# Seven block products in place of eight for some projections of a hybrid layer, with a later channel mix and a planner that tries several plans

## The chip, the cores and the metric

The kernel runs on one core of one Trainium2 chip. The metric is the device time of one execution in microseconds (us); lower is better. The profile comes from one execution, taken by the hardware profiler. TensorE is called PE (its weight loads PEld), VectorE DVE, ScalarE ACT, GpSimd POOL, SyncE SP.

## What is computed

Four stages, each added to its own input, on x of 4 batches x 1024 tokens x 256 features, all in fp32:

```
x = x + attention(layernorm(x))     # causal, one head of 256, softmax over 1024 keys
x = x + ffn(layernorm(x))           # channel mix: sigmoid(xr W_r) * (relu(xk W_k)^2 W_v)
x = x + state(layernorm(x))         # layernorm, W_in, a long convolution, silu gate z, W_out
x = x + ffn(layernorm(x))           # the same channel mix with the same weights
```

Two products matter here. In attention, the scores are (X Wm + bm) X^T, where Wm joins the weights of queries and keys; X Wm + bm are the "queries". In the state stage, z = silu(xn W_z + b_z), with W_z the second half of W_in; these are the "gates". Both are products of a 256 x 256 weight with a stream of tokens.

## The kernel before, in words

**Tiles.** A half batch j (0 to 7) is 512 tokens, a tile i (0 to 31) is 128. A stream of a half batch lies with features on partitions, in two blocks c of 128 x 512 (`cols`, L326). Tiles in SBUF come from a pool of 34 slots (L318); PSUM has 4 single banks ("bank", 128 x 512) and 2 pairs ("pair", 128 x 1024).

**The two products.** `project_columns` (L653) computes one output block e of a half batch: for c = 0, 1 one matmul of 128 x 128 weights with 128 x 512 of the stream, summed in one bank. `queries(j, e)` (L1163) evicts it with the bias on ACT or DVE; `state_gates(j, e)` (L1394) evicts it by one ACT instruction that adds the bias and applies silu. A whole batch takes two half batches x two blocks e x two c: eight matmuls. An fp32 matmul is recorded as two instructions, so x8 in the profile is four matmuls.

**The order is planned in Python.** `hybrid_kernel` does not emit instructions; it logs them in an `Order` (L49). A *unit* (`unit`, L86) is work of PE; units keep the order in which they are logged. Every other piece is an *op* (`op`, L72) with a list of engines that may do it ("ways") and a cost for each: `dve(n)` (L267), `act(n)` (L271), constants for POOL (1.27 for an addition of 128 x 512, 1.05 for a product), `columns(n, k)` (L41) for PE. `finish` (L162) first works out when each op is due (`_due`, L96, from what PE will need), then plays the program through once: an op whose inputs are there is offered at a time put off by a share of its slack (SHARE 0.2, at most MARGIN 2.5, L65); `_first` (L208) picks the op that could start first, its due time breaking ties; `_way` (L201) picks the engine that ends first; `_step` (L218) emits it. So the instruction order of DVE, ACT, POOL and SP follows from the modelled costs. The model knows PSUM banks and the DMA queue, but not the SBUF slots.

**The loop.** For each tile i, the loop at L1627 logs scores (L1203) two or three tiles ahead; DVE takes the row minimum, ACT the exponents, a write and four reads through DRAM with a DVE transposition (`turn_by_dram`, L1253) turn them into prT; then `weigh(i)` (L1314) multiplies by the values on PE (tile po) and DVE adds the result to x. `attend_prepare(j)` (L1132) normalizes a half batch and turns it into xa, and the queries and values (L1179) of the next half batch stand in between. `mix_units(i)` (L1590) puts the first channel mix (class Mix, L685: `keys`, `gates`, `values`) of half batch j at tiles i = 8 + 4j to 10 + 4j; each `values` is followed by `state_prepare(j)` (L1346: a second normalization, four ACT instructions and two POOL additions, and the turn through DRAM).

**After the loop** (L1672 on) the rest of the mix (6 and 7), the loads of the decay rows (`load_decay`, L1463: 16 DMAs of 512 KB into tiles hk), the small inputs of the convolution (`state_inputs`, L1414), the convolution (L1478), a trip of its states through DRAM (`states_out`, `states_in`), the skip products (L1527) and outputs follow. `more_gates(n)` (L1664) puts n of the 16 gate units where the order wants PE work that waits for nothing: 1, 3, 5, 1, 1, 3 and 2 of them. `mix1.transpose(7)` and `state_transpose(7)` turn the last half batch on PE, because it is needed soonest.

Of the kernel before, what the change touches and what calls it, by code (L numbers as in the profile page):

```python
# [4 lines left out]

# [7 lines left out]
F32 = mybir.dt.float32  # L13
# [6 lines left out]
P = 128  # L20
# [16 lines left out]
RPAD = P + L  # L37
AHEAD_FROM = 4
TURNED_BY_DRAM = 2

def columns(n, k=1):  # L41

    return 2 * k * max(n * 0.845e-3, 0.19)
# [5 lines left out]
class Order:  # L49
# [15 lines left out]
    SHARE, MARGIN, FRONT = 0.2, 2.5, 12.0  # L65
# [96 lines left out]
    def finish(self):  # L162
        self.due = self._due()
        self.now = self.at = 0.0
        self.free, self.ready, self.offered = {}, {}, []
        self.queue = 0.0
        self.waiting = {}
        self.psum = {kind: [0.0] * k for kind, k in self.BANKS.items()}
        for n, e in enumerate(self.log):
            if e["kind"] == "op":  # L170
                self._enter(n)
            elif e["kind"] == "known":
                self._done(e["key"], e["time"])
            elif e["kind"] == "take":
                heapq.heappop(self.psum[e["takes"]])
            else:
                self._unit(e)
        while self.offered:
            self._step()
# [28 lines left out]
    def _first(self):  # L208

        if not self.offered:  # L210
            return math.inf, None
        start, _, _, k = min(
            (self._way(time, n)[1], self.due[n], time, k)
            for k, (time, n) in enumerate(self.offered)
        )
        return start, k

    def _step(self):  # L218
# [5 lines left out]
        emit()  # L224
# [10 lines left out]
    def _unit(self, e):  # L235
# [20 lines left out]
        e["emit"]()  # L256
# [19 lines left out]
def hybrid_kernel(  # L276
# [389 lines left out]

    def project_rows(key, w, src, g, needs):
# [268 lines left out]
    def state_weights():  # L936
# [34 lines left out]
        o.op("lnb_w", ["ln"], ("POOL", 0.3, spread))  # L971
        o.unit("pb_all", 0.45, ["w_in", "lnb_w"], biases, "bank")
# [190 lines left out]
    def queries(j, e):  # L1163
        if e == 0:
# [11 lines left out]
            frees="bank",  # L1176
        )
# [212 lines left out]

    def columns_of(j):
        return [f"h{j}.T{c}" for c in range(KC)]
# [190 lines left out]

    def both(unit, j):
        unit(j, 0)
        unit(j, 1)
# [3 lines left out]
    def mix_units(i):  # L1590


        j, k = divmod(i - 8, 4) if i < NI - 1 else (6, 0)
# [31 lines left out]
    steps_of_weights = state_weights()  # L1625
    scored, valued = -1, 0
    for i in range(-2, NI):  # L1627
        first, second = mix_units(i)
        while scored < min(i + (2 if i < AHEAD_FROM else 3), NI - 1):
            scored += 1  # L1630
            scores(scored)
            if scored >= TURNED_BY_DRAM:
                turn_by_dram(scored)
        for unit in first:
            unit()
        if 0 <= i + 1 < TURNED_BY_DRAM:
            turn(i + 1)
# [3 lines left out]
        if 0 < j < 2 * NB:  # L1641
            if k == 0 and j + 1 < 2 * NB:
                attend_prepare(j + 1)
            if k == (1 if i < AHEAD_FROM else 0):
                both(queries, j)
        while valued < min(i + (3 if i < AHEAD_FROM else 4), NI - 1):
            valued += 1
            values(valued)
        for unit in second:
            unit()  # L1650
        if i == 10:
            decay_powers([f"e{i}", "la", "dtc", "dtr"])
# [4 lines left out]
        if i >= 0:  # L1657
            weigh(i)
            if i % NH == NH - 1:
                mix1.prepare(i // NH, by_hand=i == NI - 1)  # L1660

    all_gates = iter([(j, e) for j in range(2 * NB) for e in range(KC)])

    def more_gates(n):  # L1664
        for _ in range(n):
            state_gates(*next(all_gates))
# [6 lines left out]
    load_decay(1, ["po31"])  # L1673
    both(mix1.gates, 6)
    more_gates(1)
    both(mix1.values, 6)
    state_prepare(6)
    mix1.transpose(7)
    more_gates(3)
# [9 lines left out]
    more_gates(1)  # L1689
# [4 lines left out]
    more_gates(1)  # L1694
# [6 lines left out]
    more_gates(3)  # L1701
    mix_states(0)
    more_gates(2)
# [86 lines left out]
```

## Time and profile before

| | |
|---|---|
| median of 3 runs | 472.55 us (471.34 to 472.76) |
| the profiled execution, its own time | 471.39 us |
| its span (first to last instruction) | 469.2 us |
| granted TensorE clock | 1.0 |
| instructions | 6471 |
| DVE busy | 335.0 us, 886 instructions |
| ACT busy | 190.6 us, 348 instructions |
| POOL busy | 110.0 us, 119 instructions |
| memory traffic | read 40.54 MB, written 28.45 MB |

The span is the time between the first and last instruction of the program; 2.2 us of the execution lie around it. Busy time of an engine is the union of its instructions. Matmuls overlap in the pipeline, so the mean duration of one is longer than the distance to the next.

### The profile page before, as it was taken

Reading aid. Unit: us, or ns where it says so; the run is one execution under the profiler, and the core shown is the slowest. Engines: PE = TensorE matmul, PEld = TensorE weight load, DVE = VectorE, ACT = ScalarE, POOL = GpSimd, SP = SyncE. Lnnn points to the kernel's source line nnn. Section 1 sums busy time; section 2 is a strip of 40 time slices with the busy share of each in tenths; the row PEclk is TensorE's granted clock in tenths of the full one; section 3 lists DMA queues with packets and bytes.
Section 4 is the critical chain, followed back from the end, with each engine's and each line's share of the span. In section 5 each row is a group of like instructions: output and inputs, shape, how many; then the busy total and the mean of one; then the engine's idle time right before and its main releaser. Section 6 shows DMA issues by size and latency. Waiting matters only on the chain.

```text
span 469.2 us, 6471 instructions
## 1 busy us (share of the span) xinstructions
PE 463.4 (99%) x2074; PEld 317.2 (68%) x2074; DVE 335.0 (71%) x886; ACT 190.6 (41%) x348; POOL 110.0 (23%) x119
## 2 busy tenths in 40 slices
PE   8999999999999999999999999999999999999996
PEld 5765775857867757866768756474565875877765
DVE  3678879589898897786897985411577984986642
ACT  3521333335235534537442585501113454345632
POOL 3000301112402503503322374300001310243330
PEclk9999999999999999999999999999999999999999
DMA  7047864844647854628883588903032241425312
GB/s 233 26 121 216 264 174 104 243 128 143 196 115 144 228 152 136 161 77 247 258 253 88 175 270 229 342 1 80 11 113 90 80 145 45 133 92 179 92 67 67
DMA packets 84914, 69.42 MB, mean 148 GB/s; under 512 B 20161, under 2 KB 82577, under 8 KB 84881
## 3 DMA queue, kind: packets, MB, share of 16 engines
q1 hardware_dynamic: 84064, 68.76, 49.7%
q8 instruction: 16, 0.26, 0.2%
q10 hardware_dynamic: 816, 0.26, 0.2%
q14 instruction: 18, 0.14, 0.1%
HBM read 40.54 MB, written 28.45 MB: 147 GB/s over the span
## 4 chain that ended last, share of the span: by engine, by line
PE 96%; DMA 1%; DVE 1%; ACT 0%; SPq 0%; issue 0%; DVEq 0%
PE sc L1217 13%; PE po L1322 13%; PE py L1534 6%; PE pv L1189 6%; PE pc L1484 2%; PE py L1546 1%; DMA wq<-in_L_attn_a_Wq_dram 1%; PE pb L1421 1%; PE pp_a0.pq L659 1%; PE pr_g1.pv L674 1%; PE pr_g0.pr L674 1%; PE pr_f4.pr L674 1%; PE pr_f3.pr L674 1%; PE pr_f2.pr L674 1%; PE pr_f1.pr L674 1%; PE pr_f0.pr L674 1%
## 5 line engine op out<-in xcount | busy, mean ns | idle before, releaser
L1322 PE MATMUL po<-v,prT 128*128 128x256 f32 x288 | 67.9, 380 | 0.4 <-DVE prT L1275 0.3
L1217 PE MATMUL sc<-xa,q 128*128 128x512 f32 (+3 forms) x192 | 67.0, 486 | 0.0
L1322 PEld LDWEIGHTS po<-v,prT 128*128 128x128 f32 x288 | 54.2, 190 | 11.1 <-issue 2.4
L1217 PEld LDWEIGHTS sc<-xa,q 128*128 128x128 f32 x192 | 35.2, 190 | 23.6 <-issue 18.7
L1238 ACT ACTIVATE pr<-pr,nmx 128x128 f32<-128x128 f32 (+7 forms) x32 | 24.7, 772 | 57.7 <-DVE pr L1233 55.5
L1189 PE MATMUL pv<-wv,xa 128*128 128x257 f32 x128 | 32.9, 380 | 0.0
L797 POOL TENSOR_TENSOR x<-x,r_g 128x512 f32<-128x512 f32 x14 | 20.1, 1432 | 51.7 <-DVE r_g L791 41.3
L543 POOL TENSOR_TENSOR rs_f<-ve_f,minus_half 128x4 f32<-128x4 f32 x8 | 8.3, 1037 | 99.3 <-DVE ve_f L530 99.3
L797 POOL TENSOR_TENSOR x<-x,r_f 128x512 f32<-128x512 f32 x16 | 20.3, 1271 | 42.9 <-DVE r_f L791 41.7
L1189 PEld LDWEIGHTS pv<-wv,xa 128*128 128x128 f32 x128 | 24.1, 191 | 7.8 <-issue 2.9
L1534 PE MATMUL py<-xnT,wk 128*128 128x512 f32 x64 | 28.8, 596 | 0.0
L1233 DVE TENSOR_SCALAR_CACHE_REDUCE pr<-sc,v 128x128 f32<-128x128 f32 (+7 forms) x32 | 26.2, 818 | 1.1
L1556 DVE SCALAR_TENSOR_TENSOR z<-py,b_skip,z 128x512 f32<-128x512 f32 x16 | 11.0, 742 | 22.2 <-PE py L1546 22.2
L1275 DVE STREAM_TRANSPOSE prT<-pblocks 128x384 f32<-128x384 f32 (+7 forms) x30 | 23.9, 797 | 3.2 <-DMA pblocks<-exps 3.0
L1332 DVE SCALAR_TENSOR_TENSOR x<-po,rsm,x 128x256 f32<-128x256 f32 x32 | 15.5, 484 | 12.4 <-PE po L1322 10.2
L543 POOL TENSOR_TENSOR rs_g<-ve_g,minus_half 128x4 f32<-128x4 f32 x8 | 8.6, 1078 | 58.3 <-DVE ve_g L530 55.8
L1366 POOL TENSOR_TENSOR x<-x,bout_r 128x512 f32<-128x512 f32 x16 | 20.4, 1286 | 8.1 <-ACT x L1359 8.0
L1534 PEld LDWEIGHTS py<-xnT,wk 128*128 128x128 f32 x64 | 12.0, 190 | 13.7 <-issue 13.0
L543 POOL TENSOR_TENSOR rs_h<-ve_h,minus_half 128x8 f32<-128x8 f32 x8 | 13.8, 1720 | 30.0 <-DVE ve_h L532 27.3
L1359 ACT ACTIVATE x<-x,mrs_h,rs 128x256 f32<-128x256 f32 x32 | 17.2, 590 | 2.9 <-DVE rsm L1331 2.9
L1199 DVE TENSOR_TENSOR v<-pv,bv_r 128x257 f32<-128x257 f32 x32 | 13.2, 414 | 6.9 <-PE pv L1189 6.6
L712 ACT ACTIVATE xk_g<-hT_g,muk 128x512 f32<-128x512 f32 x16 | 11.1, 715 | 16.6 <-DVE hT_g L616 16.6
(429 smaller groups left out, 949.9 us busy)
## 6 DMA issues: line engine op xcount, KB each, us to landing
hk<-r_dram SPq DMA_DIRECT2D x16, 512.0 KB, 8.3
rows_g<-xn_g SPq DMA_DIRECT2D x8, 512.0 KB, 3.1
blocks_g<-rows_g SPq DMA_DIRECT2D x32, 128.0 KB, 2.7
x<-in_L_attn_a_X_dram SPq DMA_DIRECT2D x7, 512.0 KB, 4.9
rows_f<-xn_f SPq DMA_DIRECT2D x7, 512.0 KB, 3.4
blocks_f<-rows_f SPq DMA_DIRECT2D x28, 128.0 KB, 2.8
rows_h<-xn_h SPq DMA_DIRECT2D x7, 512.0 KB
blocks_h<-rows_h SPq DMA_DIRECT2D x28, 128.0 KB, 3.5
```

The lines of the kernel that those rows point to most:

```text
L543: nc.gpsimd.tensor_tensor(rs()[:, :k].rearrange("p k n -> p (k n)"), ve()[:, :k].rearrange("p k n -> p (k n)"), minus_half[:, : k * NH], A ...
L674: nc.tensor.matmul(pr()[:, j, :], lhsT=src()[:, c, ts(2 * g + j, P)], rhs=w[:, c, :], start=(c == 0), stop=(c == KC - 1),)
L797: nc.gpsimd.tensor_add(xg, xg, r()[:, ts(g, 2), :])
L1189: nc.tensor.matmul(pv()[:, : D + 1], lhsT=xaj()[:, c, ts(n, P)], rhs=wv[:, c, :], start=(c == 0), stop=(c == KC - 1),)
L1217: nc.tensor.matmul(sc()[:, k * HALF : k * HALF + w], lhsT=qh()[:, c, ts(n, P)], rhs=keys[k]()[:, c, :w], start=(c == 0), stop=(c == KC - 1),)
L1233: nc.vector.tensor_scalar(dst, src, v[2 * b + h]()[:, n, D : D + 1], None, ALU.add, ALU.min, accum_out=nmx(),)
L1238: nc.scalar.activation(p()[:, :nk], p()[:, :nk], AF.Exp, bias=nmx(), scale=-1.0, accum_out=sm())
L1275: nc.vector.transpose(dst()[:, : NH * width].rearrange("p (k m a) -> p k m a", m=NH, a=GRP), blocks().rearrange("p m (k a) -> p k m a", a= ...
L1322: nc.tensor.matmul(po()[:, :D], lhsT=src()[:, ts(n, P)], rhs=v[2 * b + n // NH]()[:, n % NH, :D], start=(n == 0), stop=(n == t),)
L1359: nc.scalar.activation(xt, xt, AF.Identity, bias=mrs()[:, 0, n : n + 1], scale=rs1()[:, n : n + 1])
L1366: nc.gpsimd.tensor_add(xg, xg, bout_r.unsqueeze(1).to_broadcast([P, 2, D]))
L1534: nc.tensor.matmul(dst()[:, ts(e, HALF)], lhsT=w_x[:, c, ts(e, P)], rhs=src()[:, c, :], start=(c == 0), stop=False,)
```

## The change

A product of 2 x 2 blocks is done with seven block products (Strassen's scheme in Winograd's form) for the queries of batches 2 and 3 (`SEVEN_FROM = 2`) and the gates of batches 1, 2 and 3 (`PLAIN = 1`). Weight blocks A(e, c) and stream blocks B(c, h), with h the half of the batch, give four weight sums S (once, on DVE) and, for each batch, four stream sums T (POOL or DVE). Each product is one unit in one bank; its eviction adds it to what is already there. A sum takes p5 twice. For the gates, silu follows as an ACT instruction of its own in SBUF. Both halves of a batch have to be there, so the second half of batches 2 and 3 is prepared four tiles earlier (i = 8 and 16), beside the first. The seven query units are put one by one between other units (`go_on`, at least 0.8 us of other units apart) from i = 11 and i = 19, and are all logged before the batch's first scores.

The mix of half batch j moves from tiles 8 + 4j .. to 10 + 4j .., so `values` 5 and all of mix 6 come after the loop. The gate steps after the loop become 0, 0, 5, 3, 3, 7 and 7: four plain units and 21 products. The planner tries 20 plans (five pairs of share and margin, four values of `WAIT`), keeps the one whose modelled end is earliest, and lets an op with an earlier due time go first if it could start on the same engine within `WAIT`. The lower bound in `columns` falls from 0.19 to 0.105.

```diff
 def columns(n, k=1):
-    return 2 * k * max(n * 0.845e-3, 0.19)
+    return 2 * k * max(n * 0.845e-3, 0.105)
...
-    SHARE, MARGIN, FRONT = 0.2, 2.5, 12.0
+    PLANS = [
+        (share, margin, wait, change)
+        for share, margin in ((0.2, 2.5), (0.1, 1.5), (0.3, 4.0), (0.2, 1.5), (0.1, 2.5))
+        for wait in (0.0, 0.08, 0.15, 0.22)
+        for change in (0.0,)
+    ]
...
     def finish(self):
-        self.due = self._due()
+        self.dues = self._due()
+        ends = []
+        for plan in self.PLANS:
+            self._run(plan, False)
+            ends.append((max(self.now, *self.free.values()), plan))
+        self.ends = ends
+        self._run(min(ends, key=lambda end: end[0])[1], True)
...
+        first = min(ways)
+        due, _, start, k = min(
+            (w[1], w[2], w[0], w[3]) for w in ways
+            if w[0] <= first[0] + self.WAIT and w[4] == first[4]
         )
-        return start, k
+        if due < first[1]:
+            return start, k
+        return first[0], first[3]
...
+    def weight_sums(t, a):
+        nc.vector.tensor_add(t[:, 0], a(1, 0), a(1, 1))
+        nc.vector.tensor_sub(t[:, 1], t[:, 0], a(0, 0))
+        nc.vector.tensor_sub(t[:, 2], a(0, 0), a(1, 0))
+        nc.vector.tensor_sub(t[:, 3], a(0, 1), t[:, 1])
+
+    def stream_sums(key, src, needs):
+        t = [lazy(lambda k=k: cols(f"T{k}_{key}")) for k in range(KC)]
...
+        for k, plus, minus in (
+            (1, lambda: b(0, 1), lambda: b(0, 0)),
+            (3, lambda: b(1, 1), lambda: b(0, 1)),
+            (2, lambda: b(1, 1), lambda: sums(1)),
+            (4, lambda: b(1, 0), lambda: sums(2)),
+        ):
...
+            o.op(
+                f"{key}.T{k}", needs + ([f"{key}.T{k - 1}"] if k in (2, 4) else []),
+                ("POOL", 1.05, partial(emit, nc.gpsimd)), ("DVE", dve(HALF), partial(emit, nc.vector)),
+            )
...
+        p = unit(1, lambda: a(0, 0), lambda: src(0)[:, 0, :], there)
+        o.op(f"{key}.u1", [f"{key}.p1"], *copies(u, p), frees="bank")
+        yield
+        p = unit(2, lambda: a(0, 1), lambda: src(0)[:, 1, :], there)
+        add("c11", 2, p, u, block(0, 0), 0, ["u1"])
+        yield
+        p = unit(6, lambda: s_of(2), lambda: t_of(2), [f"{sums_key}.T2"])
+        add("u2", 6, p, u, block(0, 1), None, ["u1"])
+        yield
+        p = unit(7, lambda: s_of(3), lambda: t_of(3), [f"{sums_key}.T3"])
+        add("u3", 7, p, block(0, 1), u, None, ["u2", "c11"])
+        yield
+        p = unit(4, lambda: a(1, 1), lambda: t_of(4), [f"{sums_key}.T4"])
+        add("c21", 4, p, u, block(1, 0), 1, ["u3"])
+        yield
+        p = unit(5, lambda: s_of(1), lambda: t_of(1), [f"{sums_key}.T1"])
+        add("c22", 5, p, u, block(1, 1), 1, ["u3"], last=False)
+        add("v12", 5, p, block(0, 1), block(0, 1), 0, ["u3"])
+        yield
+        p = unit(3, lambda: s_of(4), lambda: src(1)[:, 1, :], there)
+        add("c12", 3, p, block(0, 1), block(0, 1), None, ["v12"])
+        yield
...
-        j, k = divmod(i - 8, 4) if i < NI - 1 else (6, 0)
+        j, k = divmod(i - 10, 4)
...
-            if k == 0 and j + 1 < 2 * NB:
-                attend_prepare(j + 1)
+            if k == 0 and j == 1:
+                attend_prepare(2)
+            for n in range(3, 2 * NB):
+                if i == 4 * n - (12 if n % 2 and n > 2 * SEVEN_FROM else 8):
+                    attend_prepare(n)
...
+    both(mix1.values, 5)
+    state_prepare(5)
+    more_gates(0)
+    mix1.keys(6, 0)
+    mix1.transpose(7)
+    mix1.keys(6, 1)
     both(mix1.gates, 6)
-    more_gates(1)
+    more_gates(0)
     both(mix1.values, 6)
     state_prepare(6)
-    mix1.transpose(7)
-    more_gates(3)
     both(mix1.keys, 7)
...
     more_gates(5)
     state_transpose(7)
     state_inputs(0)
-    more_gates(1)
+    more_gates(3)
...
     state_inputs_rows(1)
-    more_gates(1)
+    more_gates(3)
...
     skip(1)
-    more_gates(3)
+    more_gates(7)
     mix_states(0)
-    more_gates(2)
+    more_gates(7)
```

The helper `add` is one DVE instruction: `tensor_add` of the bank and an SBUF tile where no bias is given, else `scalar_tensor_tensor` (bank + bias + tile), with a cost of `dve(HALF) + 0.03`.

## The prediction, made before the change was run

> **What bounds the kernel now.** I read the page's busy shares first, then the chain that ended last, then that chain in order of time, then the windows.
>
> ```profile
> PE 463.4 (99%) x2074; PEld 317.2 (68%) x2074; DVE 335.0 (71%) x886; ACT 190.6 (41%) x348; POOL 110.0 (23%) x119
> PE 96%; DMA 1%; DVE 1%; ACT 0%; SPq 0%; issue 0%; DVEq 0%
> ```
>
> PE is busy 99% of the span and 96% of the last chain. A busy PE could still be a slow PE, and the Trainium skill says so: "Perfetto Trace Analysis", section "Identifying the Most-Contended Engine", calls matmul busy time a poor measure of the distance to the limit, for which the time in weight loads is the better one. By that rule PE stands at 68%, the most contended engine is DVE at 71%, and a change that takes matmuls away and gives DVE work gains nothing. The chain in order of time decides it (start, us, what):
>
> ```profile
> 138.89 3.43 PE pp_a5.pq L659 x8
> ...
> 263.34 3.45 PE pr_f6.pr L674 x16
> 266.80 1.72 PE pp_pz0.0_2455 L659 x4
> 268.51 3.45 PE pr_f6.pv L674 x16
> 271.97 0.87 PE pt_f7.hT L641 x8
> ...
> 295.20 1.72 PE pp_pz0.4_2681 L659 x4
> 296.92 1.24 PE pt_h7.T L641 x8
> 298.15 1.85 PE pb L1421 x16
> ```
>
> Each piece starts where the one before it ends, and a matmul instruction of 512 columns takes 3.43/8 = 1.72/4 = 0.429 us in every kind of unit, in attention and after it. So matmuls go through at a fixed rate whatever happens to the weight loads (0.19 us each, inside 0.429); I go by the row: a matmul less is time less, wherever PE is not made to wait. PE hardly waits for data now: outside the first 12 us I find 0.3 us at 65.2 (for prT) and 0.37 us in pt_h7 (1.24 us instead of the 0.87 of pt_f7).
>
> **What is removed.** Each batch done by seven products loses one matmul of 512 columns, that is two instructions: 2 x 0.429 = 0.86 us. Two batches of queries and three of gates: 5 x 0.86 = 4.29 us, all on the path. Nothing else of PE's work changes in amount; the mix, the preparation and the gates are moved.
>
> **What is added, and where.** These groups price it (busy, mean ns):
>
> ```profile
> L791 DVE SCALAR_TENSOR_TENSOR r_f<-r_f,pr_f3.pv 128x512 f32<-128x512 f32 x2 | 1.4, 690 | 1.4 <-PE pr_f3.pv L674 1.4
> L1577 DVE TENSOR_TENSOR x<-x,pr_pyo1.0_2971 128x512 f32<-128x512 f32 x1 | 0.7, 689 | 1.0 <-PE pr_pyo1.0_2971 L674 1.0
> L797 POOL TENSOR_TENSOR x<-x,r_f 128x512 f32<-128x512 f32 x16 | 20.3, 1271 | 42.9 <-DVE r_f L791 41.7
> ```
>
> - *Evictions.* Seven additions from a bank per batch, 0.69 us each: 4.8 us, 24 us for five batches, all on DVE. They replace two DVE evictions of queries (0.75 each). ACT gives up evictions and gets u1 and silu in SBUF: level. DVE goes to about 335 + 23 + weight sums (8 of 128x128, at 0.29 as the mask addition of that size, 2.3) = 360 us, 77%: no bound over the whole.
> - *Stream sums*, 20 of 128x512 with two SBUF inputs. The skill ("GPSIMD Engine Reference", section "Engine selection") says to keep elementwise additions on VectorE, GpSimd being about twice as slow. The row agrees in the ratio (1.27 us), but POOL is busy 23% of the time: on POOL they are 25 us that nothing waits for, on DVE 14 us more where it has least room. I go with POOL for most. The plan believes 1.05 us, so a T2, which follows T1, comes some 0.5 us later than planned; units p1 and p2 and those put between lie in front of p6.
> - *Banks.* Seven products in a row come every 0.86 us and are evicted at 0.69 us, with p5 evicted twice: 8 x 0.69 = 5.5 us against 6.0 us. Four banks cover the delay. In the stretch after the convolution DVE is nearly empty (below). Cost nothing; if DVE were 3 us behind there, banks would run out and PE would wait that long.
> - *Silu* now waits for a DVE addition instead of a product. Behind it in ACT's queue stand the normalizations of half batch 7 and the convolution's small work; ACT is busy 5.1 of 10 us at 290 to 300 and less after: 0 for those, and up to the lateness of that addition otherwise. Its table is still loaded once, since the gates come after the last exponential.
> - *Bound in `columns`, 20 plans.* They alter only orders, by a model. Between -0.3 us (the wait at 65.2 goes) and +1; I take 0.
>
> **Attention.** The windows of 10 us (columns: window and its length, PE, PEld, DVE, ACT, POOL, clock, DMA share and GB/s):
>
> ```profile
> 100.00:110.00 10.00, 10.00 (x26) 4.75 (x25) 9.22 (x15) 3.26 (x5) 1.90 (x1) 1.00 0.34 104
> 110.00:120.00 10.00, 10.00 (x107) 8.20 (x106) 9.37 (x33) 5.54 (x11) 1.02 (x1) 1.00 0.44 134
> ...
> 160.00:170.00 10.00, 10.00 (x34) 6.12 (x33) 9.30 (x20) 4.61 (x8) 1.46 (x2) 1.00 0.70 194
> ...
> 320.00:330.00 10.00, 10.00 (x29) 4.03 (x28) 2.73 (x4) 2.75 (x4) 0.00 (x0) 1.00 0.29 82
> ```
>
> The seven products of batch 2 fall at about 98 to 118 us, those of batch 3 at about 165 to 190. DVE is busy 27.7 of 30 us in 95 to 125 and 26.3 of 32 us in 163 to 195. To each comes 4.8 us of evictions and about 5.1 us of the earlier preparation (four statistics of 0.59, some of the normalizations at 0.42, two transpositions at 0.65, the small ones): 9.9 us. Over by 7.6 us and 4.2 us. What goes late first is what has room: prT. The DVE timeline and the chain show it for tile 13, the one with the least room of its neighbours:
>
> ```profile
> 108.86 0.96 DVE L1275 STREAM_TRANSPOSE prT<-pblocks 128x768 f32<-128x768 f32 x1
> ```
> ```profile
> 118.83 2.79 PE po L1322 x12
> ```
>
> Written at 109.8, first used at 118.8: 9 us; paired in the same way, tiles 12 to 31 have 5.9 to 15 us, and tile 15 (used at 131.8) 6.0. So 7.6 us of lateness fits but for 1.6 us if all of it falls on tile 15, and if the order puts evictions first, as due times from PE's needs do. Both ends: 0, or 7.6 + 4.2 = 11.8 us if no cover could be used. I take 0.2, near the lower end, because every row of cover is near or over the lateness. Queries must be complete before the scores of tiles 16 and 24; the last product is logged a tile ahead. The earlier preparation also takes one write and four reads past SP's queue and the DMA engines, at a DMA share of 0.34 to 0.44: hidden. The mix two tiles later takes its evictions, POOL additions and DMAs along, with inputs that are ready earlier than before: 0. The query weight sums (1.2 us of DVE near 22 us) stand before tiles 2 and 3, whose prT has 1.6 and 2.4 us of cover: 0; without it they would cost their 1.2.
>
> **After the loop** the filler changes, and this is where I expect to lose.
>
> - *pt_f7* needs the last tile's x, its statistics and POOL's power: inputs ready at 268.7, 5.3 us after the last po ended at 263.3. Before, 8.6 us of units lay between; now values 5 and half of keys 6, 3.45 + 1.72 = 5.2 us. Between 0 and 1.5 (values 5 bring DVE work into the gap): I take 0.2.
> - *pt_h7*: from the end of values 7 (288.3) to its inputs (297.2) are 8.9 us, against a filler of five gate units, 8.6 us: the 0.37 us above. Now four plain units and one product, 4 x 1.72 + 0.86 = 7.7 us: 0.86 us less. In the chain POOL's second addition waits 0.8 us behind another and the statistics 1.6 us behind two transpositions, so another order could save it. Between 0 and 1.2 (with T sums on POOL in front of its power): I take 0.5 more.
> - *h6*: `state_inputs(0)` needs the stream of half batch 6 through DRAM. Before, it was there at 292.9, 20.9 us after values 6 ended at 272.0, and needed at 298.1. Now values 6 come later: keys, gates and values 7 (10.3), the filler (7.7) and pt_h7 (0.9) leave 18.9 us, plus the waits above. That chain was put off by its slack before, but it shares the DMA queue with the 16 loads of hk (median 8.3 us to landing). Between 0 and 3: I take 0.3.
> - Behind the convolution the filler before `mix_states(0)` grows from 3.43 + 5.15 to 3.43 + 6.0 us: less exposed than now. Slots: not in the planner's model; four T tiles and one u come while hk holds 16, and z of batch 1 is not yet there. A wait for a slot would stop POOL first, which is idle at 310 to 330: 0.
>
> **Sum.** -4.29 + 0.2 + 0.2 + 0.5 + 0.3 = -3.1 us. The profiled execution took 471.39 us (span 469.2 and 2.2 around it), so 468.3 on its own terms, a span near 466.1. It lies 1.16 us under the median of 472.55, within the spread of the three; on the median, 469.5 us.
>
> **The rivals.**
> - *All of it arrives*, and the plan avoids the waits: 472.55 - 4.3 = 468.2. For it: PE had no waits before under the same model, and the best of 20 plans is taken. Against: the three gaps after the loop are shorter than the chains they cover.
> - *Given back after the loop*: pt_f7 1.5, pt_h7 1.2 and h6 1 to 3 at their upper ends, 3.7 and more: near 472.3, no change. For it: hk loads and half batches 5 and 6 share the queue and POOL. Against: each chain had idle time in it.
> - *DVE becomes the bound in attention, slower.* If bank evictions stand behind preparation work in DVE's order, PE's four banks fill and the lateness reaches PE. With 8 of the 11.8 us: 472.55 - 4.3 + 8 = 476.3. It turns the sign once more than 4.3 us reach PE, that is, when usable cover in each window falls from 6 us or more to under 3.7 (11.8 - 2 x 3.75 = 4.3). Against: prT's cover, and POOL for the sums.
> - *It doesn't do what it says*: a product of one matmul costing more than 0.43 per instruction for lack of accumulation; the transpositions and scores show no such price; included in the first range.
>
> **Chances.** Likeliest (469.5) 0.47; all of it 0.25; given back 0.13; slower 0.15. A measurement tells 0.3%, 1.4 us, from no change. Faster: 0.47 + 0.25 = 0.72; same 0.13; slower 0.15. The range reaches from the full gain with the waits of before gone and the runs' own spread of 1.2 under their median (466.8) to the lower half of the slower case (474.0), leaving out under 0.2.
>
> **What would show it.** Right: 80 matmul instructions of queries and gates fewer and 70 of products in their place, 2064 in all; PE busy near 459; waits in pt_f7 and pt_h7 of some tenths; DVE near 360 us with 90% and more at 95 to 195 and no PE wait there. Wrong: PE idle before po or a product's bank in 95 to 195 (rival three); pb waiting for `blocks_h` for microseconds (rival two); the additions on DVE well over 0.69 us; sums on DVE; a start-to-start of the products over 0.43 us.

## The result, and the profile after

| | before | after |
|---|---|---|
| median, same chip | 472.39 us (471.00 to 472.76, 5 runs) | 475.40 us (474.47 to 476.08, 5 runs) |
| ratio | | 1.0069, 95% interval 1.0047 to 1.0091 |
| the profiled execution, its own time | 471.39 us | 474.82 us |
| its span | 469.2 us | 473.0 us |
| granted TensorE clock | 1.0 | 0.992 |

The change is slower by 0.7%, 3.0 us, where 3.1 us of gain were forecast; the time lies outside the range of the forecast (466.8 to 474.0). The page of the kernel after: busy time, the granted clock in 40 slices of 11.8 us, and the shares of the chain that ended last.

```profile
PE 462.1 (98%) x2064; PEld 315.1 (67%) x2064; DVE 375.6 (79%) x931; ACT 192.7 (41%) x354; POOL 121.9 (26%) x128
...
PEclk9999999999999999999999998899999999999999
...
PE 74%; DVE 14%; DMA 6%; ACT 2%; issue 2%; SPq 1%; POOL 0%; DVEq 0%; ACTq 0%
```

PE had 96% of that chain before. Now DVE and DMA hold 20%, and the two slices from 284 to 307 us show a lower clock, just where PE stood still. The chain in order of time, at that place:

```profile
289.26 0.71 DVE xnT L651
289.97 0.89 DVE mrs_h L587 x2
290.87 0.62 DVE xnT L651
291.49 1.95 DVE xn_h L593 x2
...
293.48 1.54 PE pt_h7.T L676 x6
```

By the starts of its instructions, PE is idle from 288.23 to 292.30 and again from about 292.65 to 293.48, until half batch 7 is normalized. That takes three steps: POOL's power (`rs_h`, one over the root of the variances), DVE's shift (`mrs_h`, made of mean and power, 128 x 4) and the normalized rows (`xn_h`, 128 x 256 each). Before, they stood like this (timeline of before: start, us, engine, line, what):

```profile
294.33 1.65 POOL L543 TENSOR_TENSOR rs_h<-ve_h,minus_half 128x8 f32<-128x8 f32 x1 [1.90 <-DVE ve_h L532]
...
296.01 0.23 DVE L552 SCALAR_TENSOR_TENSOR mrs_h<-rs_h,mv_h 128x4 f32<-128x4 f32 x2 [1.76 <-POOL rs_h L543]
296.17 1.05 DVE L558 TENSOR_SCALAR xn_h<-x,mv_h,rs_h 128x256 f32<-128x256 f32 x3
```

From the powers' end (295.98) to the last normalized row: 1.2 us. After, the powers end at 288.33 and the rows are there at 293.43: 5.1 us. The timeline of after shows what stands between and what runs beside:

```profile
286.68 1.65 POOL L578 TENSOR_TENSOR rs_h<-ve_h,minus_half 128x8 f32<-128x8 f32 x1 [0.87 <-ACT z L1596]
...
288.30 1.26 POOL L1521 TENSOR_TENSOR x<-x,bout_r 128x512 f32<-128x512 f32 x1
289.26 0.71 DVE L651 STREAM_TRANSPOSE xnT<-blocks_h 128x512 f32<-128x512 f32 x1 [2.05 <-DMA blocks_h<-rows_h]
289.52 1.26 POOL L733 TENSOR_TENSOR T_zs<-xnT 128x512 f32<-128x512 f32 x1
289.90 0.97 DVE L587 SCALAR_TENSOR_TENSOR mrs_h<-rs_h,mv_h 128x4 f32<-128x4 f32 x2
290.74 1.26 POOL L733 TENSOR_TENSOR T_zs<-xnT,xnT 128x512 f32<-128x512 f32 x1
290.79 0.70 DVE L651 STREAM_TRANSPOSE xnT<-blocks_h 128x512 f32<-128x512 f32 x1
...
291.42 2.01 DVE L593 TENSOR_SCALAR xn_h<-x,mv_h,rs_h 128x256 f32<-128x256 f32 x2
...
291.97 2.59 POOL L1521 TENSOR_TENSOR x<-x,bout_r 128x512 f32<-128x512 f32 x2
292.30 0.66 PE L676 MATMUL pt_h7.T<-ident,xn_h 128*128 128x128 f32 x2 [3.91 <-DVE xn_h L593]
```

Two things make the 3.9 us more. First, DVE waits until 289.26 for the reads of half batch 6 through DRAM and transposes them (`xnT`, twice) in the order of its queue, ahead of the shifts and of the normalization: about 2.1 us that before had been over by then. Second, two shifts take 0.97 us instead of 0.23, and two normalizations 2.01 us where three took 1.05 (before, two of them took 0.73): about 2.0 us. Each of these two groups ends about when a POOL addition ends: 290.87 beside 290.78, 293.43 beside 293.3 (half of 2.59 from 291.97). Against this, 0.3 us are saved, since ACT normalizes one tile more. The same slowing shows at tile 31's half batch, before `pt_f7`:

```profile
258.52 1.26 POOL L924 TENSOR_TENSOR x<-x,r_f 128x512 f32<-128x512 f32 x1
...
258.60 1.20 DVE L587 SCALAR_TENSOR_TENSOR mrs_f<-rs_f,mv_f 128x4 f32<-128x4 f32 x1
```

**The ledger of the span** (after less before, from the starts of PE's instructions): five products less, -4.29; an earlier start of the first projection (11.68 instead of 12.38), -0.70; three old waits gone (65.2, 178 and the 0.37 in pt_h7), -1.0. Against it: 0.73 at 92.2 us (the first query product waits for DVE's transposition of xa), 0.73 at 114.5 (po13 behind DVE), 0.73 in pt_f7, 4.07 + 0.83 at the last transposition, and 2.7 of slow clock behind it (the convolution's inputs, pb, take 3.54 instead of 1.85 us in the chain). Sum: -6.0 + 9.8 = +3.8, for a measured +3.9.

### The profile page after: what moved, and what is told of

Its sections match the earlier page's. It is cut to its first block, busy times and chain, and to the rows that moved or that the text cites. A ratio compares the mean times of both kernels' runs of the same rounds, so it can differ in the third digit from the quotient of the medians.

```text
span 473.0 us, 6537 instructions
## 1 busy us (share of the span) xinstructions
PE 462.1 (98%) x2064; PEld 315.1 (67%) x2064; DVE 375.6 (79%) x931; ACT 192.7 (41%) x354; POOL 121.9 (26%) x128
## 4 chain that ended last, share of the span: by engine, by line
PE 74%; DVE 14%; DMA 6%; ACT 2%; issue 2%; SPq 1%; POOL 0%; DVEq 0%; ACTq 0%
PE po L1477 9%; PE sc L1372 9%; PE py L1729 6%; PE pv L1344 5%; PE p_zs L750 4%; PE p_qs L750 3%; PE pc L1679 2%; DMA blocks_h<-rows_h 1%; DMA rows_h<-xn_h 1%; DVE xr_f L842 1%; DVE pr L1388 1%; PE pb L1616 1%; DVE xk_f L842 1%; PE py L1741 1%; DMA wq<-in_L_attn_a_Wq_dram 1%
## 5 line engine op out<-in xcount | busy, mean ns | idle before, releaser
L578 POOL TENSOR_TENSOR rs_a<-ve_a,minus_half 128x4 f32<-128x4 f32 x7 | 7.1, 1010 | 65.7 <-DVE ve_a L565 65.7
L1521 POOL TENSOR_TENSOR x<-x,bout_r 128x512 f32<-128x512 f32 x16 | 20.7, 1309 | 8.1 <-ACT x L1514 8.1
```

What stands on the lines that cost most here:

```text
L578: nc.gpsimd.tensor_tensor(rs()[:, :k].rearrange("p k n -> p (k n)"), ve()[:, :k].rearrange("p k n -> p (k n)"), minus_half[:, : k * NH], A ...
L1521: nc.gpsimd.tensor_add(xg, xg, bout_r.unsqueeze(1).to_broadcast([P, 2, D]))
```

## Theories and experiments

**Theory H (holding).** A POOL addition that reads SBUF holds up DVE instructions that work between SBUF and SBUF; the change puts such additions (`shifted`, L1521, of half batches 5 and 6, and the new stream sums) where DVE normalizes the last half batches. **Rival W (work and order).** DVE merely has too much to do there, and the filler is shorter; POOL is a bystander. **Rival C (clock).** The wait is what it is, the low clock behind it makes the loss. I came to H only after the runs e1 to e8. Ratios are to before on the same chip.

**e1_dust and e2_filler: is it the filler or the clock?**

```diff
 # e1_dust
     more_gates(5)
+    keep_going(19)        # idle matmuls of 512 columns in bf16, at no cost in the plan
     state_transpose(7)
 # e2_filler: gate steps 0, 0, 9, 2, 2, 6, 6 in place of 0, 0, 5, 3, 3, 7, 7
```

> 19 idle bf16 matmuls of 512 columns (about 4 us of PE at full clock) stand ahead of the transpositions of half batch 7 (pt_h7), at a modelled cost of nothing, so that the order of all engines stays that of the changed kernel; they compute nothing that is used. Theory (a wait of 4.1 us at pt_h7 for the normalization of half batch 7, and after it a TensorE clock that has fallen because PE stood still, which costs about 3.4 us more between pt_h7 and the first product behind it): the wait is filled and not shortened, the clock stays at 1.0, and 2.5 to 3.4 us come back: 472 to 473 us. Rival (the slow stretch behind pt_h7 is data that comes late, not the clock): no change, 475.4 us, and the intervals of 0.83 us between pairs of the small products pb stay.

> Nine gate steps instead of five ahead of pt_h7, and 2, 2, 6, 6 behind in place of 3, 3, 7, 7: 3.4 us more of PE work that waits for nothing. The same arithmetic. Theory (filler shorter than the chain of half batch 7): the wait falls from 4.1 to under 1.5 us and the clock does not fall, 6 to 7.5 us come back: 468 to 469.5 us. Rival (DVE has too much work in this stretch, whatever the order of PE's units): the stream sums and evictions of the four products more come into the same stretch, the wait stays at 3 to 4 us: 474 to 476 us.

e1: 474.59 us, 1.0070 (1.0055 to 1.0085), as the change itself. The idle matmuls (4.26 us from 289.08) keep the clock at 0.998 and pb takes 1.92 us, yet PE then waits 0.9 us for `bT`, which stands on DVE behind four stream sums and starts at 299.98 (in after, behind the same sums, at 299.06). Nothing is won: the slow clock was spent in the shadow of a late DVE. C falls. e2: 477.91 us, 1.0153 (1.0110 to 1.0197), slower than both of its expectations; its trace is of an execution of 481.35 us. The wait at pt_h7 is gone, but the plan moved work and PE waits 5.8 us before pt_f7 and 2.2 before a product. More filler at one place isn't a cure.

**e3_sums: the stream sums at another place.** The sums of batch 1 are logged right behind the loop, those of batches 2 and 3 after the fifth product of the batch before.

> The stream sums of batch 1's gates are logged right behind the loop instead of with its first product, those of batches 2 and 3 after the fifth product of the batch before, so that they do not run while half batch 7 is normalized. Nothing else changes. Theory with contention (sums on POOL slow the normalizations on DVE to 1.0 us each from 0.42, and delay them): the wait at pt_h7 falls by 1 to 2 us, and with it some of the slow clock: 472 to 474 us. Theory without it (the chain is held up by DVE standing at the transposition of half batch 6 for its DMA): under 0.5 us, 475 us.

476.62 us, 1.0114 (1.0099 to 1.0129), no better than the change; the waits at the last transposition are 4.26 and 1.27 us. The sums alone are not it: with them away, three additions L1521 (290.30, 291.52, 292.75) lie on the shifts and the normalizations.

**e4 to e8: which part of the change loses?**

```diff
 # e4_order_alone: the later mix and the planner, no seven products
-PLAIN = 1
-SEVEN_FROM = 2
+PLAIN = 4
+SEVEN_FROM = 4
 # gate steps 0, 0, 5, 2, 2, 4, 3
 # e5_old_mix: all products, the order of before (mix at 8 + 4j), sums late, steps 1, 3, 10, 2, 2, 5, 2
 # e6_queries: the order of before, PLAIN = 4.   e8_gates: the order of before, SEVEN_FROM = 4
 # e7_plans_alone: the order of before, PLAIN = 4, SEVEN_FROM = 4
```

> The later mix, the new order behind the loop, the 20 plans and the new bound, but every projection with eight products: gate units 0, 0, 5, 2, 2, 4, 3 (16 plain ones). Theory (products only shorten the filler at pt_h7 and add sums there; the order would nearly do): against the kernel before, a wait of 0 to 2 us at pt_h7: 472.5 to 475 us. Rival (the seven products are the loss, the order none): 472 to 472.8 us. Other rival (the later mix alone makes the loss, since half batch 6 then runs into half batch 7): the same wait of 3 to 4 us and the slow clock: 478 to 480 us.

> All seven-product batches, the 20 plans and the new bound, but the channel mix at tiles 8 + 4j and the order behind the loop as in the kernel before (mix 5 and half of mix 6 inside the loop); gate steps 1, 3, 10, 2, 2, 5, 2, which give the same PE work at each place as before (ten products for five units); stream sums of a batch logged after the fifth product of the batch before. Theory (the later mix makes the loss: it pushes half batches 5, 6 and 7 together behind the loop): 2 to 4 us under the kernel before. Rival (the products' DVE work in the stretch behind the loop makes it, whatever the mix): DVE over 90% busy from 270 to 300 us, waits at products or pt_h7, 0 to 4 us over the kernel before.

> Seven products for the queries of batches 2 and 3 alone; gates by 16 plain units; mix and order behind the loop as in the kernel before; 20 plans, new bound. PE has 1.72 us less. Theory (attention has room for the added DVE work): 0.7 to 1.7 us under the kernel before. Rival (DVE becomes the bound in attention): PE waits at po or at a product between 95 and 260 us, and 0 to 4 us over.

> No seven products anywhere, mix and orders as in the kernel before; only the 20 plans, the waiting for an earlier due time and the lower bound in the cost of small matmuls are left of the change (the weight sums are computed and not used). Theory (the planner is harmless): within 0.5 us of the kernel before. Rival (the plan that its model likes best is worse on the chip than the old one): 1.5 to 4 us over, by waits that the model does not show.

> Seven products for the gates of batches 1 to 3 alone, queries plain, mix as in the kernel before, gate steps 1, 3, 10, 2, 2, 5, 2, 20 plans. PE has 2.57 us less. Theory (later mix makes the loss): 1 to 2.5 us under the kernel before. Rival (DVE behind the loop has no room for six to ten products with their sums): waits of 1 to 4 us at pt_h7 or in the products, 0 to 3 us over.

| run | us | ratio (95%) | PE waits over 0.3 us after 20 us |
|---|---|---|---|
| e4 order alone | 476.58 | 1.0110 (1.0086 to 1.0134) | 0.6 at 65, 0.4 at pt_f7, 3.1 at pt_h7 |
| e5 old order, all products | 476.80 | 1.0124 (1.0104 to 1.0145) | 1.2 at 109, 0.7 at 188, 0.9 at 258, 1.2 in products, 2.1 in pt_h7, 1.7 at 315 |
| e6 queries alone | 471.58 | 1.0006 (0.9995 to 1.0017) | 0.9 at 109, 0.7 at 187, 0.3 at 271 |
| e7 planner alone | 469.81 | 0.9971 (0.9962 to 0.9981) | none |
| e8 gates alone | 477.32 | 1.0133 (1.0117 to 1.0148) | 0.9 at 277, 2.5 in products, 2.1 in pt_h7, 1.7 at 315 |

The planner with its bound gains 1.4 us, where neither expectation saw a gain. e4 lies between two of its expectations, e5 and e8 lost more than either of theirs, and e6 gained nothing, as its rival had it. The order without a single product loses as much as the products of the gates do without the new order, and both mainly around one place, the normalization of half batch 7. They don't add up (together the change loses only 3 us), which suggests a shared cause there but does not show it: in e8 a stream sum and evictions stand in DVE's order ahead of the shifts as well. In e4 DVE is busy 343.6 us against 335.0; if each DVE instruction is compared with the same one while POOL is idle, 21 us of this are excess against 13 before, which is the whole difference, so W has no work to point at. In its trace the shifts run beside two POOL additions:

```profile
291.05 2.49 POOL L1521 TENSOR_TENSOR x<-x,bout_r 128x512 f32<-128x512 f32 x2
291.12 1.29 DVE L587 SCALAR_TENSOR_TENSOR mrs_h<-rs_h,mv_h 128x4 f32<-128x4 f32 x2 [1.76 <-POOL rs_h L578]
```

A third addition L1521 (285.37, 1.28 us) stands in POOL's queue between the two additions to x that the statistics wait for. This gave theory H.

**e9 to e11: POOL's additions put behind the normalization, by the plan.** `h4.o` to `h6.o` get the normalized rows of half batch 7 as a need; in e10 so do the transpositions of half batch 6.

```diff
 # e9_pool_free (sums as in e3), e11_order_pool_free (on e4)
-                f"{key}.o{g}", [f"{key}.y{2 * g}", f"{key}.y{2 * g + 1}", "bin"],
+                f"{key}.o{g}", [f"{key}.y{2 * g}", f"{key}.y{2 * g + 1}", "bin"]
+                + ([f"h7.xn{n}" for n in range(NH)] if 4 <= j < 7 else []),
 # e10_pool_free_turn_late, besides
-                names[c], [f"{key}.r{j}" for j in range(P // GRP)],
+                names[c], [f"{key}.r{j}" for j in range(P // GRP)]
+                + ([f"h7.xn{n}" for n in range(NH)] if key == "h6" else []),
```

> All of the change, with three needs altered: the POOL additions of the skip rows of half batches 4 to 6 (shifted) wait for the normalized rows of half batch 7, the sums of batch 1 are asked for right behind the loop and those of batches 2 and 3 after the fifth product of the batch before (as in e3_sums, 476.6 us, PE waits of 4.26 and 1.27 us before the last transposition). So POOL has nothing to add while DVE normalizes half batch 7. Theory (a POOL addition of two SBUF inputs holds up DVE instructions that read and write SBUF: shifts of 0.15 us become 1.0 to 1.2, normalizations of 0.41 become 1.0 to 1.4): shifts 0.16 each and normalizations 0.42, the wait falls by about 2 us to 2 to 3 us, of which 1.6 us stand for DVE's transposition that waits for half batch 6's reads; time about 473 to 474 us. Rival (DVE has simply too much to do there, and the additions only run at the same time): the durations stay near 1 us and the wait stays at 4 us or more, time 476 to 477.

> As e9_pool_free, and the two DVE transpositions of half batch 6 after its trip through DRAM wait for the normalized rows of half batch 7, so that nothing that waits for a DMA stands before these on DVE. Theory (the wait at the last transposition is two causes in a row, 1.6 us behind the reads and 2 to 2.5 us of stretched instructions): the wait before the last transposition falls to under 1 us and its chain from the powers to the last normalization is back at 1.2 us, as before the change; the transpositions come 1.4 us later and PE may wait for them up to 1 us before the next convolution inputs. Time about 472 us. Rival (too much work on DVE): wait of 3 us or more, time over 475.

> e4_order_alone (the later mix and the planner, no seven products, 476.6 us, PE waits 3.13 us before the last transposition) with the POOL additions of the skip rows of half batches 4 to 6 waiting for the normalized rows of half batch 7. Theory (POOL additions hold up DVE): the shifts take 0.16 us each instead of 0.65, the wait falls to 1.5 us or less, time about 473 to 474. Rival (the shorter filler and work on DVE, no matter what POOL does): wait stays near 3 us, time about 476.5.

e9: 476.25, 1.0115 (1.0094 to 1.0135). e10: 475.52, 1.0094 (1.0078 to 1.0111). By their expectations both speak for W. But the traces show that the edit does not do what I meant: a need orders the plan, it is no dependency of the data, so POOL ran the additions as soon as its powers were done, right onto the normalization. e9 therefore shows half batch 6 with POOL idle and half batch 7 under five additions in a row:

```profile
283.20 1.05 DVE L593 TENSOR_SCALAR xn_h<-x,mv_h,rs_h 128x256 f32<-128x256 f32 x3
...
292.93 6.32 POOL L1521 TENSOR_TENSOR x<-x,bout_r 128x512 f32<-128x512 f32 x5
293.09 1.20 DVE L587 SCALAR_TENSOR_TENSOR mrs_h<-rs_h,mv_h 128x4 f32<-128x4 f32 x2
...
294.21 3.91 DVE L593 TENSOR_SCALAR xn_h<-x,mv_h,rs_h 128x256 f32<-128x256 f32 x3
```

The same three instructions take 1.05 and 3.91 us; each ends 0.15 us after an addition, and PE waits 2.9 us between the transpositions that each of them frees (the trace is of an execution of 478.42 us, 2.2 over the median of e9). e11 is 472.21, 1.0015 (1.0007 to 1.0023), 4.4 us better than e4 and better than H expected, in part for another reason: its shifts still take 1.29 us, but with no addition between those to x the powers end 5.7 us after values 7 instead of 9.0, and PE doesn't wait there at all.

**e12: products only where DVE has room.** The order of before, `PLAIN = 2`, no queries, gate steps 1, 3, 6, 2, 2, 5, 3; the stream sums need the normalized rows of half batch 7.

> The order of before with the 20 plans and the lower bound in columns (e7_plans_alone, 0.9971 of before), with seven products for the gates of batches 2 and 3 alone; their stream sums wait until half batch 7 is normalized. Gate steps after the loop 1, 3, 6, 2, 2, 5 and 3: eight plain units and two products before the last transposition (8.6 us, as before). Two batches save 2 x 0.86 = 1.7 us of PE. Theory (seven products are worth their matmuls where DVE has room, as after the normalization of half batch 7, and lose only where their sums and evictions meet that normalization): all arrives, 468.1 us, ratio 0.9935. Rival (the products lose wherever they stand, for example because their evictions hold up the convolution's small DVE work): 470 us or more, ratio 0.997 or above.

470.47 us, 0.9981 (0.9972 to 0.9990): faster than before, but with 1.7 us of matmuls less no faster than e7 (0.9971, intervals overlap). That is what the rival expected (470 us or more). PE waits 0.6 at 273.8 (for ACT's copy behind pt_f7) and 0.7 at 278.0 (for the mixing by DVE), and nothing else over 0.2.

**e13 and e14: POOL truly idle.** A small POOL instruction that reads the normalized rows stands in front of the additions: a dependency of the data.

```diff
 # on e9 (e13_pool_idle) and on e10 (e14_pool_idle_turn_late)
+            o.op("h7.mark", parts, ("POOL", 0.2, lambda: nc.gpsimd.tensor_tensor(
+                mark(), xn()[:, :, 0], xn()[:, :, 1], ALU.add)))
-                + ([f"h7.xn{n}" for n in range(NH)] if 4 <= j < 7 else []),
+                + (["h7.mark"] if 4 <= j < 7 else []),
```

> As e9_pool_free (476.25 us), with a small POOL addition that reads the normalized rows of half batch 7, behind which the POOL additions of half batches 4 to 6 stand; now POOL is idle while DVE normalizes. Theory (POOL additions hold up DVE): shifts of half batch 7 back at 0.23 for two and normalizations at 0.42 each (e9: 1.20 and 3.91 for three), PE's waits of 2.9 us in the last transposition fall to under 0.5 us, and the time by about 2.5 to 473.7 us; the wait of 3.3 us before the transposition of tile 31's half batch (another place) stays. Rival (too much work on DVE, at whatever speed): durations stay near 1 us, waits stay, 476 us.

> As e10_pool_free_turn_late (475.52 us), with the same small POOL instruction. Theory: from the powers' end to the last normalization 1.2 us instead of 5.4, the three waits of 1.06, 1.07 and 1.40 us in the last transposition go, the clock does not fall behind them, time about 471.5 us. Rival: over 475 us.

e13: 473.91 us, 1.0063 (1.0045 to 1.0082); e9 had 1.0115. e14: 471.17, 0.9998 (0.9983 to 1.0013); e10 had 1.0094. As H expected, to 0.3 us. The timeline of e13:

```profile
291.06 0.24 DVE L587 SCALAR_TENSOR_TENSOR mrs_h<-rs_h,mv_h 128x4 f32<-128x4 f32 x2
291.22 1.05 DVE L593 TENSOR_SCALAR xn_h<-x,mv_h,rs_h 128x256 f32<-128x256 f32 x3
...
292.42 0.20 POOL L1516 TENSOR_TENSOR mark<-xn_h 128x4 f32<-128x4 f32 x1 [1.39 <-DVE rs L1533]
...
292.57 3.76 POOL L1529 TENSOR_TENSOR x<-x,bout_r 128x512 f32<-128x512 f32 x3
```

POOL's small instruction and the additions now follow the normalization. The durations are back, and PE has no wait of 0.15 us or more in the last transposition, with the same work on all engines and, from values 7 to the normalized rows, the same DVE instructions in the same order as in e9. W falls for this place. What e13 still loses is 3.1 us before pt_f7, where a stream sum (260.79, 1.26 us on POOL) lies on the shift (1.22 us) and the normalization.

**e17: the whole change, with POOL idle at both places.** As e14, with such an instruction for tile 31's half batch in front of the additions of values 5 (`f5.x`), and all stream sums of the gates behind that of half batch 7.

> As e14_pool_idle_turn_late (471.17 us), the whole change; besides, the POOL additions of values 5 (f5.x) stand behind a second such POOL instruction that reads the normalized rows of tile 31's half batch, and all the stream sums of the gates stand behind that of half batch 7. Theory (the same cause at both transpositions): the shift of that half batch takes 0.16 us instead of 1.2, PE's waits of 1.8 us there go or fall under 0.5, and the time to 469.5 us; what is left above 466.9 are the waits in attention. Rival (that wait is work and order): over 471 us.

469.64 us, 0.9965 (0.9953 to 0.9977): all products of the change, and now faster than before. It is not shown to be faster than the planner alone (e7, 0.9971; the intervals overlap), though 4.3 us of matmuls are gone. The shift before pt_f7 takes 0.16 us and the wait there is gone:

```profile
258.91 0.16 DVE L587 SCALAR_TENSOR_TENSOR mrs_f<-rs_f,mv_f 128x4 f32<-128x4 f32 x1
```

The span is 466.9 us, PE busy 459.6. The windows of 15 us at the loss, before, after and then e17 (columns as in the prediction):

```profile
285.00:300.00 15.00, 15.00 (x61) 7.81 (x59) 6.89 (x21) 7.94 (x14) 7.02 (x6) 1.00 1.00 314
```

```profile
285.00:300.00 15.00, 10.57 (x36) 3.95 (x35) 12.78 (x21) 7.60 (x14) 12.38 (x10) 0.77 0.85 280
```
```profile
285.00:300.00 15.00, 14.31 (x63) 5.51 (x62) 12.74 (x23) 6.43 (x12) 12.58 (x11) 1.00 0.93 304
```

DVE and POOL are as busy in both (12.8 and 12.4 against 12.7 and 12.6 us); PE gets 10.6 us in one and 14.3 in the other. Before, DVE and POOL had 6.9 and 7.0 us there. Here the load does not decide, but what lies on what. What e17 still waits: 1.3 us in attention and 0.6 at the last transposition.

**e15, e16 and e18: which products are worth it.** e15 is the change's order and queries, but gates of batches 2 and 3 alone (steps 0, 0, 6, 3, 3, 6, 4), POOL idle at half batch 7. e16 is e12 with POOL idle. e18 is e15 without the queries' products, POOL idle at both places.

> The change with its order and seven products for the queries of batches 2 and 3, but for the gates of batches 2 and 3 only (eight plain units before), gate steps 0, 0, 6, 3, 3, 6 and 4 after the loop, the stream sums of the gates and the POOL additions of half batches 4 to 6 behind the normalization of half batch 7 by the same small POOL instruction. PE has 3.4 us less work than before; the filler before the last transposition is 4 plain and, in place of the rest, two plain units, 10.3 us in all. Theory: no wait at the last transposition; what stays are the waits in attention (0.7 to 1.5 us) and before the transposition of tile 31's half batch (0.7 to 3), so 469.5 to 471. Rival (the later mix loses by itself, 6.6 us): over 474 us.

> e12_last_batches (470.47 us; seven products for the gates of batches 2 and 3 in before's order; PE waits of 0.6 and 0.7 us at 274 to 278 us and 0.2 at the last transposition) with the stream sums and the POOL additions of half batches 5 and 6 behind the normalization of half batch 7 by the small POOL instruction. Theory (the two waits stand behind POOL additions of half batch 5 that stretch the shift by one token and the mixing on DVE): 469 us or less. Rival (they come from the plan's order): 470.5 us.

> As e15_change_late_products (469.64 us), without the seven products of the queries and with the POOL additions of values 5 behind the normalization of tile 31's half batch. PE has 1.7 us more work than e15, and the waits in attention (0.8, 0.3 and 0.8 us in e15) go if they come from the earlier preparation and the queries' evictions: 469.5 us, the same. If the queries' products are worth their matmuls: 471.4 us.

e15: 469.64, 0.9969 (0.9959 to 0.9980). e16: 470.92, 0.9993 (0.9984 to 1.0002), no better than e12: waits of 0.5 and 0.5 us at 273 and 277 remain and one of 1.0 us at pbt is new. H as I put it for those two waits fails. e18: 469.08, 0.9957 (0.9942 to 0.9972), the lowest median of all, with two of the five batches of the change: no PE wait over 0.3 us behind the one at 64.6 (0.7). The waits of e15 in attention (0.8, 0.3 and 0.8 us) are gone with the queries' products, and are about as long as their matmuls, 1.7 us. The intervals of e17, e15, e7 and e18 overlap; which of them is best is not shown, and so not either that any product is worth its place beside the planner.

## Why the prediction was wrong, point by point

- *What is removed, -4.29 us*: right. 2064 matmul instructions, 0.43 us each from start to start, and in e17, where little stands in the way, PE busy at 459.6 against the 459 forecast.
- *The rule of weight loads that I set aside* ("gains nothing"; the page names the share of peak FLOPs beside it, which I left out): for the time of a matmul I read the rows rightly, as the line above shows. The outcome was still nearer to the rule than to my forecast, for another reason than a full DVE: DVE was not busy throughout, but late at a few places.
- *Evictions at 0.69 us, banks enough*: right (0.69, and 0.745 with a bias). They read PSUM, and POOL's additions don't touch them (0.691 us with and without).
- *Stream sums on POOL, "25 us that nothing waits for"*: wrong twice. DVE took 13 of 20; and the sums on POOL cost DVE its time beside them. DVE came to 375.6 us where I forecast 360; in e17 it is 362.6. Of these 13 us, most (11 us, by the comparison made for e4) is time in which DVE was held.
- *The rule I weighed.* I set the Trainium skill's advice to keep elementwise additions on VectorE against POOL's 77% of idle time, and looked no further than the ratio of the two durations. Another page, "SBUF — State Buffer", section "Who interferes with whom", says what was needed: a DVE instruction with two SBUF inputs, or in a 2-port performance mode, which it says `tensor_scalar` can enter when its operands allow, contends with a GpSimd instruction that reads SBUF, and whichever comes first blocks the other for its whole length. The traces agree, with numbers (last section). Even the trace of before had it: beside a POOL addition its shifts took up to 1.22 us and its normalizations up to 1.38, where nobody waited.
- *The moved mix "0"*: wrong. It takes the POOL additions of half batches 5 and 6 along, from where POOL's pauses lay to the normalization of half batch 7. e4, which has this with the new order behind the loop and the planner, but no product, loses 5.2 us; I priced the operations that were moved, and not what they would lie on.
- *pt_h7 0.5 and h6 0.3*: **the step that failed.** Measured 7.6 us, 4.9 of PE standing and 2.7 at a low clock (the latter hidden behind DVE, by e1). I saw the filler 0.86 us shorter and a range to 1.2 and 3, but took the chain from powers to rows at before's 1.2 us; it became 5.1. From values 7 to the powers' end nothing changed, 7.8 us in both. Of the 3.9 us more, about 2.0 are held shifts and normalizations, and about 2.1 the transpositions of half batch 6 in front of them, the first of which waits for its DMA; I had named two such transpositions in before's chain (1.6 us), and put no time on their coming later. For the holding, experiments show it: 2.3 us of time come back when POOL is idle (e9 to e13), and 4.4 where the transpositions stand behind the normalization in both (e10 to e14). For the transpositions the trace of after shows it; in e13 they are through at the powers' end and cost nothing, and no run moves them alone in the order of after.
- *pt_f7 0.2*: 0.73, from the same cause (shift 1.20 us); mechanism missed, place right.
- *Attention 0.2*: 1.5 us. Rival three had the place but not the manner: prT's cover held (5.6 us and more for nearly all tiles from 12 on), but xa of half batch 5, prepared earlier, comes late for the first query product, and po13 waits for DVE once.
- *20 plans 0*: too low, e7 gains 1.4 us.
- *The rival "given back after the loop"* was the right one in place, with 0.13; its sum of 3.7 us had no term for DVE slowing down, so it ended at no change.

Open: whether the model could be taught the holding (not tried), what in e17 keeps the products' 4.3 us from showing beside e7, and what keeps e12 and e16 from their full gain.

## What to carry to other kernels

An idle engine is not free if its instructions hold up those of the one that is late: before work is moved to POOL, or along with a stage, look at which DVE instructions of the kinds below will lie beside it, and who waits for those. A planner's order is only as good as its model: here it had a duration for each instruction, and did not know that two of them exclude each other. To keep an engine quiet at a place, a need in the plan isn't enough; it takes a dependency that the hardware sees.

## What the runs showed of the hardware

From the traces of after, e9, e13 and e17 together, the medians of a DVE instruction that begins while a POOL addition of 128 x 512 is running, against the same one with POOL idle. Held: the shift (128 x 4, two SBUF inputs) 0.99 against 0.153 us, to 1.23 at most; the normalization (`TENSOR_SCALAR`, 128 x 256) 0.91 against 0.41, to 1.44; the mixing of tokens (128 x 512, two SBUF inputs) 1.53 against 0.74; a stream sum on DVE 1.64 against 0.68. Whatever was left of the addition when they began, 0.16 to 1.25 us, they end a fixed time behind its end: shifts 0.02 us, normalizations 0.15 to 0.19, mixing and sums 0.55 to 0.58. Not held, though SBUF to SBUF too: statistics (0.395 both ways) and transpositions (0.70 both ways), so H was worded too widely; nor anything with an operand in PSUM (0.691 and 0.744 against 0.691 and 0.745). POOL's own `pow` holds nothing (shift 0.154 beside it). POOL is held in turn: in after, two of its stream sums beside those of DVE took 1.72 and 1.60 us instead of 1.27.

After 4 us of standing still PE ran at half speed: transpositions 213 ns apart instead of 110, pb's pairs 0.85 us instead of 0.43, from 292.3 to about 298 us, where the profile gives a granted clock of 0.5 (291.6 to 298.4); the Trainium skill ("TensorE: Matmul & The Clock Gate", "Part 1: The HAM clock gate") gives half the clock for a cold array as well.
